# Layer 3 of a fused graph network: another score product, other stage order, held instructions

## The chip, the core and the metric

The kernel runs on one core of one Trainium2 chip. The core has a matrix engine (PE, whose weight loads are listed apart as PEld), a vector engine (DVE), a scalar engine for activations (ACT), a general engine (POOL, also called GpSimd) and a queue engine (SP) that issues DMAs. Each engine takes its instructions in order; they wait for each other by semaphores. Working memory is SBUF with 128 partitions; PE writes to PSUM, which has eight banks of 512 f32 values per partition. The metric is device time in microseconds (us).

## The reference

Four layers work on x of 128 graphs x 64 nodes x 256 features, each of them as x + layer(relu(layernorm(x))). Layer 0 is graph convolutions and small LSTMs, layer 1 attention over edges, layer 2 a dense graph layer with two batch norms, and layer 3, which the change is about, dense attention inside each graph:

```python
Wh = jnp.einsum('bnf,fo->bno', h, W)
a1, a2 = (a[:Fout, 0], a[Fout:, 0])
s1 = Wh @ a1
s2 = Wh @ a2
e = s1[:, :, None] + s2[:, None, :]
e = jnp.where(e >= 0, e, ALPHA * e)
e = jnp.where(adj_matrix[None] == 0, -jnp.inf, e)
attention = jax.nn.softmax(e, axis=-1)
h_prime = jnp.einsum('bij,bjo->bio', attention, Wh)
```

A score of nodes i and j is the sum of two half scores, s1 of the row's node and s2 of the column's node.

## The kernel before

The 8192 nodes are cut into 16 chunks (NCH) of 512: four tiles (i) of 128 nodes, which are two graphs each. All four layers run in one program; layer 3 begins when the second batch norm of layer 2 is complete. Up to that point everything is as it is after the change, but for a few tables made in late_tables during layer 0: wext (the weights W of layer 3 with W a1 as column 257), wa2 (W a2, repeated over 64 columns), eye and the mask.

A chunk passes through these functions in layer 3:

- **fetch**: a DMA on SP's queue brings the residual from memory into the tile xts[n].
- **scale_o**: POOL applies the second batch norm to layer 2's product (two instructions per chunk); the result o lies with features on the partitions.
- **second_norm**: a generator in two stages. PE turns o into nodes on the partitions (eight transposes), DVE adds it to the residual and takes the statistics of the layer norm (four pairs of bn_stats and bn_aggr). Then the roots: for chunks 1 and 2 by ACT and DVE, for all others by POOL, which also writes the normed h. Chunk 0 has its own first_norm, in halves.
- **features**: PE turns h back (eight transposes), ACT writes the relu of it as hT, in two halves.
- **project3**: hT times wext, two f32 products for each of four tiles; ACT copies each result to wh (256 values and the half score s1).
- **dense_scores**: the half scores s2 of all nodes of a graph, spread over the partitions, come from wa2 and hT (four products with 64 weight columns; the two graphs of a tile go to the two halves of the partitions). DVE adds s1, applies the leaky relu, adds the mask and takes the negative maximum (four instructions), ACT takes exp tile by tile with row sums den, DVE the reciprocal of den.
- **turn**: PE transposes the four tiles of e; DVE copies the first graph's half into fields[n % 2] and ACT the second's.
- **dense_values**: four products of the field with wh, then four DVE instructions that scale by 1/den and add the residual, then the store on SP's queue (the last chunk is stored in two halves).

PSUM is used in two kinds of buffers in this layer: "bank" (one bank, four buffers) for project3, dense_scores and turn, and "pair" (two banks, two buffers) for second_norm, features and dense_values. A buffer is used again when its last readers are done.

The order of instructions on an engine is made by a scheduler when the program is built: it takes them by readiness and by their place in the code. late(ins) holds one instruction behind the one that was traced just before it on the same engine; instructions without it may be moved. In layer 3, before the change, only chunk 0 and parts of chunks 1 and 2 are held. The main loop of iteration n runs second_norm(n+2), scale_o(n+4), features(n+1), half of project3(n), turn(n-1), the other half, dense_scores(n) and dense_values(n-1).

Of the kernel before, what the change touches and what calls it, by code (L numbers as in the profile page):

```python
# [9 lines left out]
F32 = mybir.dt.float32  # L10
# [21 lines left out]
def gnn_stack_kernel(ctx: ExitStack, tc: tile.TileContext, a: dict, out: bass.AP):  # L32
# [168 lines left out]

    tab2 = ctx.enter_context(tc.tile_pool(name="tab2", bufs=1))
    bdH = tab2.tile([P, P], F32, tag="bdH", name="bdH")
    wext = tab2.tile([P, 2, D + 1], F32, tag="wext", name="wext")
    wa2 = tab2.tile([P, 2, T], F32, tag="wa2", name="wa2")
    mask3 = tab2.tile([P, T], F32, tag="mask3", name="mask3")

    def late_tables():
        with ExitStack() as setup:
# [7 lines left out]
            late(nc.vector.tensor_scalar(mask3, adj2, 0.0, NEG, ALU.is_equal, ALU.mult))  # L217
            yield

            eye = s2.tile([P, T], F32, tag="eye", name="eye")  # L220
            for h in range(2):
                r = slice(h * T, (h + 1) * T)
                nc.vector.tensor_copy(eye[r, :], ident[r, r])
            an = s2.tile([P, T], F32, tag="an", name="an")
            anT = s2.tile([P, T], F32, tag="anT", name="anT")
            nc.vector.tensor_tensor(an, adj2, eye, ALU.add)
# [1276 lines left out]
    with ExitStack() as l2:  # L1503
# [407 lines left out]
        def second_norm(n):  # L1911

            xt, v = xts[n], hs[n][0]
            o = os3.pop(n)
            p = pair_bank()
            for i in range(4):
                for c in range(2):
                    k = (i % 2 * 2 + c) * P
                    ins = nc.tensor.transpose(p[:, i // 2, k : k + P], o[:, c, i * P : (i + 1) * P], ident)  # L1919
# [12 lines left out]
            nm = stat.tile([P, 4], F32, tag="ln_nm", name="ln_nm")  # L1932
            if n < 3:
                keep(nc.scalar.activation(rs, mv[:, :, 1], AF.Sqrt, bias=eps))
                keep(nc.vector.reciprocal(rs, rs))
                keep(nc.vector.scalar_tensor_tensor(nm, mv[:, :, 0], -1.0, rs, ALU.mult, ALU.mult))
            else:
                nc.gpsimd.tensor_scalar(rs, mv[:, :, 1], 1e-5, None, ALU.add)
                nc.gpsimd.tensor_tensor(rs, rs, half_power, ALU.pow)
                nc.gpsimd.tensor_tensor(nm, mv[:, :, 0], rs, ALU.mult)  # L1940
                nc.gpsimd.tensor_scalar(nm, nm, -1.0, None, ALU.mult)
            h = norms[n] = as_tokens(v)
            for i in range(4):
                if n > 2 or i > 1:
                    nc.gpsimd.tensor_scalar(
                        h[:, i, :], xt[:, i, :], rs[:, i : i + 1], nm[:, i : i + 1], ALU.mult, ALU.add
                    )
                else:
                    nc.scalar.activation(
                        h[:, i, :], xt[:, i, :], AF.Identity, bias=nm[:, i : i + 1], scale=rs[:, i : i + 1]  # L1950
                    )

        def features(n):

            h = norms.pop(n)
            p = pair_bank()
            for i in range(4):
                for c in range(2):
                    k = i % 2 * 2 * P + c * P
                    nc.tensor.transpose(p[:, i // 2, k : k + P], h[:, i, c * P : (c + 1) * P], ident)  # L1960
            hT = hT3[n] = t2.tile([P, 2, CHUNK], F32, tag="aggT2", name="hT3")
            for b in range(2):
                nc.scalar.activation(
                    hT[:, :, b * 256 : (b + 1) * 256].rearrange("p c (i t) -> p i c t", i=2),
                    p[:, b, :].rearrange("p (i c t) -> p i c t", i=2, c=2),
                    AF.Relu,
                )

        def project3(n, tiles):

            if n not in att3:
                wh = t4.tile([P, 4, D + 1], F32, tag="wh", name="wh", bufs=3)
                att3[n] = [wh, None, None]
            for i in tiles:
                p = bank()
                for k in range(2):
                    mm(
                        p[:, : D + 1],
                        hT3[n][:, k, i * P : (i + 1) * P],
                        wext[:, k, :],  # L1980
                        k == 0,
                        k == 1,
                    )
                nc.scalar.copy(att3[n][0][:, i, :], p[:, : D + 1])

        def dense_scores(n):

            wh, hT = att3[n][0], hT3.pop(n)
# [7 lines left out]
            nc.vector.tensor_tensor(  # L1996
                e,
                p[:, : 4 * T].rearrange("p (i t) -> p i t", t=T),
                wh[:, :, D:].to_broadcast([P, 4, T]),
                ALU.add,  # L2000
            )
            nc.vector.scalar_tensor_tensor(e, e, 0.2, e, ALU.mult, ALU.max)
            nc.vector.tensor_tensor(e, e, mask3.unsqueeze(1).to_broadcast([P, 4, T]), ALU.add)
            nmx = stat.tile([P, 4], F32, tag="nmx3", name="nmx3")
            nc.vector.tensor_reduce(nmx, e, AX.X, ALU.max, negate=True)
# [5 lines left out]
            nc.vector.reciprocal(den, den)  # L2011
            att3[n][1:] = [e, den]

        def turn(n):
# [1 line left out]
            e = att3[n][1]  # L2016
            p = bank()
            for i in range(4):
                nc.tensor.transpose(p[:T, i * P : (i + 1) * P], e[:, i, :], ident)
            f = att3[n][1] = fields[n % 2]  # L2020
            for h in range(2):
                r = slice(h * T, (h + 1) * T)
                (nc.scalar.copy if h else nc.vector.tensor_copy)(
                    f[r, :, r], p[:T, :].rearrange("p (i j) -> p i j", i=4)[:, :, r]
                )

        def dense_values(n):
            wh, f, den = att3.pop(n)
            xt = xts.pop(n)
            p = pair_bank()  # L2030
            for i in range(4):
                mm(p[:, i // 2, i % 2 * D : (i % 2 + 1) * D], f[:, i, :], wh[:, i, :D])
            for i in range(4):
                nc.vector.scalar_tensor_tensor(
                    xt[:, i, :],
                    p[:, i // 2, i % 2 * D : (i % 2 + 1) * D],
                    den[:, i : i + 1],
                    xt[:, i, :],
                    ALU.mult,
                    ALU.add,  # L2040
                )
# [5 lines left out]
            if n < NCH - 1:  # L2047
                nc.sync.dma_start(out=token_tiles(out, n), in_=xt)

        for n in range(4):  # L2050
            fetch(n)
        for n in range(3):
            scale_o(n)
        start = first_norm()
        next(start)
        second = second_norm(1)
        next(second)
        for _ in start:
            pass
        project3(0, (0, 1))  # L2060
        for _ in second:
            pass
        scale_o(3)
        for n in range(NCH + 1):
            if 4 <= n + 4 < NCH:
                fetch(n + 4)
            if n + 2 < NCH:
                for _ in second_norm(n + 2):
                    pass
            if n + 4 < NCH:  # L2070
                scale_o(n + 4)
            if n == 0:
                project3(0, (2, 3))
                dense_scores(0)
                features(1)
                continue
            if n + 1 < NCH:
                features(n + 1)
            if 0 <= n < NCH:
                project3(n, (0, 1))  # L2080
            if n >= 1:
                turn(n - 1)
            if 0 <= n < NCH:
                project3(n, (2, 3))
                dense_scores(n)
            if n >= 1:
                dense_values(n - 1)

# [1 line left out]
def _laid_out(i):  # L2090
# [65 lines left out]
```

## Time and profile before

| what | value |
|---|---|
| median of 3 runs | 1998.3 us (1996.55 to 1998.84) |
| profiled execution, its own time | 2002.48 us |
| its span | 2000.6 us |
| PE, PEld busy | 1952.1 us (98%), 1390.4 us (69%) |
| DVE, ACT, POOL busy | 1309.3 us (65%), 1139.8 us (57%), 439.3 us (22%) |
| layer 3's own part | from about 1846 us of the span to its end |

The profile is taken in one execution, which takes a little longer than the median of the runs. "Busy" is the time in which an engine has an instruction under way. A view of the profile that is cut to a stage shows what that stage is limited by, while the shares above are means over four layers. In the chain of waits each piece is the work that the end of the program was waiting for at that time. In the timeline, brackets tell how long the engine was idle before an instruction and who released it.

### The profile page before, as it was taken

Reading aid. Unit: us, or ns where it says so; the run is one execution under the profiler, and the core shown is the slowest. Engines: PE = TensorE matmul, PEld = TensorE weight load, DVE = VectorE, ACT = ScalarE, POOL = GpSimd, SP = SyncE. Lnnn points to the kernel's source line nnn. Section 1 sums busy time; section 2 is a strip of 40 time slices with the busy share of each in tenths; the row PEclk is TensorE's granted clock in tenths of the full one; section 3 lists DMA queues with packets and bytes.
Section 4 is the critical chain, followed back from the end, with each engine's and each line's share of the span. In section 5 each row is a group of like instructions: output and inputs, shape, how many; then the busy total and the mean of one; then the engine's idle time right before and its main releaser. Section 6 shows DMA issues by size and latency. Waiting matters only on the chain. (4 is left out here: it accounts for less than half of the span.)

```text
span 2000.6 us, 25691 instructions
## 1 busy us (share of the span) xinstructions
PE 1952.1 (98%) x9502; PEld 1390.4 (69%) x9502; DVE 1309.3 (65%) x2468; ACT 1139.8 (57%) x2137; POOL 439.3 (22%) x574
## 2 busy tenths in 40 slices
PE   9999999999999999999999999999999999999998
PEld 7777478866678854888666888666556775444786
DVE  8764676565475567665645655657766877886775
ACT  4343766565465547665555655567665556691544
POOL 3000031030030011310300200356654510000562
PEclk9999999999999999999999999999999999999999
DMA  8522000010010053001001000531334741022112
GB/s 271 166 69 85 0 22 1 1 42 0 1 43 0 1 190 104 22 1 43 0 1 42 1 0 17 201 105 58 117 121 152 295 154 44 0 84 84 43 54 74
DMA packets 63870, 135.61 MB, mean 68 GB/s; under 512 B 6657, under 2 KB 41345, under 8 KB 61441
## 3 DMA queue, kind: packets, MB, share of 16 engines
q1 hardware_dynamic: 59808, 124.33, 18.3%
q0 software_dynamic: 3328, 9.44, 1.3%
q8 instruction: 75, 1.23, 0.3%
q10 hardware_dynamic: 608, 0.20, 0.1%
q14 instruction: 51, 0.41, 0.1%
HBM read 87.55 MB, written 46.40 MB: 67 GB/s over the span
## 5 line engine op out<-in xcount | busy, mean ns | idle before, releaser
L761 ACT ACTIVATE gate<-gate,bias 128x256 f32<-128x256 f32 (+2 forms) x368 | 247.2, 678 | 183.6 <-DVE gate L777 100.1
L733 PE MATMUL pa<-xop,sih 128*128 128x256 f32 (+2 forms) x1056 | 342.4, 417 | 9.1 <-DVE gate L787 8.9
L733 PEld LDWEIGHTS pa<-xop,sih 128*128 128x128 f32 x1056 | 198.8, 190 | 82.5 <-issue 20.3
L733 PE MATMUL pc<-xop,wih 128*128 128x256 f32 (+2 forms) x736 | 251.1, 423 | 0.0
L777 DVE TENSOR_TENSOR gate<-pb,gate 128x256 f32<-128x256 f32 (+2 forms) x184 | 87.3, 475 | 224.7 <-PE pb L733 151.3
L733 PE MATMUL pa<-lstm_h,shh 128*128 128x256 f32 (+1 forms) x672 | 212.7, 398 | 0.0
L733 PEld LDWEIGHTS pc<-xop,wih 128*128 128x128 f32 x736 | 139.8, 190 | 51.2 <-issue 22.5
L1101 ACT ACTIVATE lr<-pair 128x1024 f32<-128x1024 f32 x128 | 124.1, 1021 | 70.5 <-PE pair L1091 40.8
L792 DVE TENSOR_TENSOR gate<-pc,gate 128x256 f32<-128x256 f32 (+2 forms) x184 | 87.4, 475 | 112.8 <-PE pc L733 112.5
L733 PEld LDWEIGHTS pa<-lstm_h,shh 128*128 128x128 f32 x672 | 127.7, 190 | 30.2
L733 PE MATMUL pc<-lstm_h,whh 128*128 128x256 f32 (+1 forms) x448 | 141.8, 398 | 0.0
L776 ACT COPY gate<-pa 128x256 f32<-128x256 f32 (+2 forms) x184 | 75.9, 412 | 91.4 <-PE pa L733 91.0
L1060 PE MATMUL bank<-wlv,hT 128*128 128x260 f32 x480 | 122.2, 398 | 0.0
L787 DVE TENSOR_TENSOR gate<-pa,gate 128x256 f32<-128x256 f32 (+2 forms) x184 | 87.2, 474 | 43.3 <-PE pa L733 42.7
L761 ACT ACTIVATE gate<-pa,bias 128x256 f32<-128x256 f32 (+2 forms) x184 | 93.7, 509 | 31.3 <-PE pa L733 29.8
L1060 PEld LDWEIGHTS bank<-wlv,hT 128*128 128x128 f32 x480 | 87.3, 192 | 32.8 <-issue 15.7
L781 ACT COPY gate<-pa 128x256 f32<-128x256 f32 (+2 forms) x184 | 75.0, 408 | 52.6 <-PE pa L733 51.6
L733 PE MATMUL pa<-xop,wih 128*128 128x256 f32 (+1 forms) x320 | 101.6, 399 | 2.8 <-ACT xop L714 2.7
L733 PE MATMUL pb<-xop,wih 128*128 128x256 f32 (+1 forms) x320 | 100.4, 398 | 0.0
L733 PEld LDWEIGHTS pc<-lstm_h,whh 128*128 128x128 f32 x448 | 85.1, 190 | 20.1
L505 POOL TENSOR_TENSOR shh<-whh 128x512 f32<-128x512 f32 x6 | 8.2, 1367 | 384.9 <-DMA whh<-in_WhhT 326.6
L784 ACT COPY gate<-pc 128x256 f32<-128x256 f32 (+2 forms) x136 | 57.7, 424 | 52.4 <-PE pc L733 51.9
(372 smaller groups left out, 3968.0 us busy)
## 6 DMA issues: line engine op xcount, KB each, us to landing
field<-keep SPq DMA_DIRECT2D x4, 2304.0 KB
wih<-in_WihT SPq DMA_DIRECT2D x8, 1024.0 KB
xres<-in_x SPq DMA_DIRECT2D x16, 512.0 KB
xa<-xres POOLq DMA_DIRECT2D x16, 512.0 KB
dense<-field SPq DMA_DIRECT2D x4, 2048.0 KB
xin<-xb SPq DMA_DIRECT2D x16, 512.0 KB
h<-xb SPq DMA_DIRECT2D x16, 512.0 KB
xin<-in_x SPq DMA_DIRECT2D x15, 512.0 KB
```

What stands on the lines that cost most here:

```text
L505: keep(nc.gpsimd.tensor_tensor(o, x, y, op))
L733: ins = nc.tensor.matmul(p[:, : self.N], weights[kind, self.phase](k, q), x[k], start=first_ and kind == "ih", stop=kind == "hh" or not se ...
L761: nc.scalar.activation(out, in_, AF.Tanh if q == 2 else AF.Sigmoid, bias=bias[:, self.w - 1, 2 * q + j : 2 * q + j + 1],)
L776: nc.scalar.copy(blk[0, 0], pa[:, :N])
L777: nc.vector.tensor_tensor(blk[0, 0], pb[:, :N], blk[0, 0], ALU.add)
L781: nc.scalar.copy(blk[1, 0], pa[:, :N])
L784: (nc.vector.tensor_copy if not self.t and self.w > 1 else nc.scalar.copy)(blk[1, 1], pc[:, :N])
L787: nc.vector.tensor_tensor(blk[1, 1], pa[:, :N], blk[1, 1], ALU.add)
L792: nc.vector.tensor_tensor(blk[1, 0], pc[:, :N], blk[1, 0], ALU.add)
L1060: ins = nc.tensor.matmul(o, hTs[n][:, k, i * P : (i + 1) * P], wlv[:, k, cols], start=k == 0, stop=k == 1)
L1101: nc.scalar.activation(lr, p, AF.Relu)
```

## The change

It touches layer 3 alone. dense_scores gets s2 another way: wext has a further column (W a2), so wh carries both half scores; a new stage, spread, lets POOL multiply s2 of each node by a unit matrix (eye), and one product with same_graph (ones inside each graph's block) puts the sums on all partitions. The main loop is rewritten: the normed chunks run three ahead instead of two, values follow two behind instead of one, and nearly all first instructions of a group on PE, and the DVE instructions, are held with late(). The sqrt of chunks 1 and 2 is issued with the statistics, ahead of the generator's second yield; a single exp of one column is put behind the sqrt of chunk 2; the reciprocal of den goes from dense_scores to dense_values; chunk 13's values are cut in halves around the end of the loop.

```diff
-    wext = tab2.tile([P, 2, D + 1], F32, tag="wext", name="wext")
-    wa2 = tab2.tile([P, 2, T], F32, tag="wa2", name="wa2")
+    wext = tab2.tile([P, 2, D + 2], F32, tag="wext", name="wext")
+    same_graph = tab2.tile([P, P], F32, tag="same_graph", name="same_graph")
+    eye = tab2.tile([P, T], F32, tag="eye", name="eye")
...
+            nc.vector.memset(same_graph, 0.0)
             for h in range(2):
                 r = slice(h * T, (h + 1) * T)
                 nc.vector.tensor_copy(eye[r, :], ident[r, r])
+                nc.vector.memset(same_graph[r, r], 1.0)
...
-                nc.vector.tensor_copy(wext[:, c, D:], p[:, 2 * c : 2 * c + 1])
-                nc.vector.tensor_copy(wa2[:, c, :], p[:, 2 * c + 1 : 2 * c + 2].to_broadcast([P, T]))
+                nc.vector.tensor_copy(wext[:, c, D:], p[:, 2 * c : 2 * c + 2])
...
         def second_norm(n):
...
-                    if n < 3 and i + c == 0:
+                    if i + c == 0:
                         late(ins)
             flat = xt.rearrange("p i d -> p (i d)")
-            keep = late if n < 3 else lambda ins: ins
-            keep(nc.vector.tensor_tensor(flat, p.rearrange("p b d -> p (b d)"), flat, ALU.add))
+            keep = late
+            late(nc.vector.tensor_tensor(flat, p.rearrange("p b d -> p (b d)"), flat, ALU.add))
+            yield
...
             rs = stat.tile([P, 4], F32, tag="ln_rs", name="ln_rs")
+            if n < 3:
+                keep(nc.scalar.activation(rs, mv[:, :, 1], AF.Sqrt, bias=eps))
             yield
...
         def features(n):
...
+                    if i + c == 0:
+                        late(ins)
...
+        def spread(n):
+
+            wh = att3[n][0]
+            hT3.pop(n)
+            across = spreads[n] = t4.tile([P, 4, T], F32, tag="across", name="across")
+            late(nc.gpsimd.tensor_tensor(
+                across,
+                wh[:, :, D + 1 :].to_broadcast([P, 4, T]),
+                eye.unsqueeze(1).to_broadcast([P, 4, T]),
+                ALU.mult,
+            ))
+
         def dense_scores(n):
...
-            for k in range(2):
-                hv = hT[:, k, :].rearrange("p (i o t) -> p o i t", o=2, t=T)
-                for h in range(2):
-                    mm(p[h * T : (h + 1) * T, : 4 * T], wa2[:, k, :], hv[:, h], k == 0, k == 1)
+            late(nc.tensor.matmul(p[:, : 4 * T], same_graph, across.rearrange("p i t -> p (i t)"), start=True, stop=True))
...
         def turn(n):
...
-                nc.tensor.transpose(p[:T, i * P : (i + 1) * P], e[:, i, :], ident)
+                ins = nc.tensor.transpose(p[:T, i * P : (i + 1) * P], e[:, i, :], ident)
+                if not i:
+                    late(ins)
...
+        def dense_values(n, tiles=(0, 1, 2, 3)):
...
+            if tiles[0] == 0:
+                results[n] = pair_bank()
+            p = results[n]
+            for i in tiles:
+                ins = nc.tensor.matmul(
+                    p[:, i // 2, i % 2 * D : (i % 2 + 1) * D], f[:, i, :], wh[:, i, :D], start=True, stop=True
                 )
+                if i in (0, tiles[0]):
+                    late(ins)
+            if tiles[0] == 0:
+                late(nc.vector.reciprocal(den, den))
+            for i in tiles:
+                late(nc.vector.scalar_tensor_tensor(
...
         for n in range(4):
             fetch(n)
             scale_o(n)
+        begun = first_norm()
+        next(begun)
+        coming = second_norm(1)
+        next(coming)
+        next(coming)
+        run(begun)
         project3(0, (0, 1))
+        run(coming)
+        coming = second_norm(2)
+        next(coming)
+        project3(0, (2, 3))
+        spread(0)
+        next(coming)
+        loaded = stat.tile([P, 1], F32, tag="loaded", name="loaded")
+        late(nc.scalar.activation(loaded, eps, AF.Exp))
+        features(1)
+        dense_scores(0)
+        run(coming)
+        scale_o(4)
+        coming = second_norm(3)
+        next(coming)
+        for n in range(1, NCH + 2):
+            if n + 3 < NCH:
+                fetch(n + 3)
+            if 1 < n <= NCH:
+                dense_scores(n - 1)
+            next(coming, None)
+            if n < NCH:
+                project3(n, (0, 1, 2, 3))
+                spread(n)
+            run(coming)
             if n + 4 < NCH:
                 scale_o(n + 4)
+            if n == NCH - 1:
+                dense_values(n - 2, (0, 1))
+                turn(n - 1)
                 continue
+            if n == NCH:
+                dense_values(n - 3, (2, 3))
+            if n == 1:
+                features(2)
+            if n >= 2:
+                dense_values(n - 2)
+            if n <= NCH:
+                turn(n - 1)
+            if n + 3 < NCH:
+                coming = second_norm(n + 3)
+                next(coming)
+            if 1 < n < NCH - 1:
+                features(n + 1)
```

run(stage) advances a generator to its end. The instructions of dense_scores on DVE, and the copies of turn, are held as well.

More of the change, by code (lines that the diff above doesn't have):

```diff
@@ L218, in late_tables @@
             yield
-            eye = s2.tile([P, T], F32, tag="eye", name="eye")
+            nc.vector.memset(same_graph, 0.0)
             for h in range(2):
@@ L1933, in second_norm @@
             if n < 3:
-                keep(nc.scalar.activation(rs, mv[:, :, 1], AF.Sqrt, bias=eps))
                 keep(nc.vector.reciprocal(rs, rs))
@@ L1959, in features @@
                     k = i % 2 * 2 * P + c * P
-                    nc.tensor.transpose(p[:, i // 2, k : k + P], h[:, i, c * P : (c + 1) * P], ident)
+                    ins = nc.tensor.transpose(p[:, i // 2, k : k + P], h[:, i, c * P : (c + 1) * P], ident)
+                    if i + c == 0:
+                        late(ins)
             hT = hT3[n] = t2.tile([P, 2, CHUNK], F32, tag="aggT2", name="hT3")
@@ L1971, in project3 @@
             if n not in att3:
-                wh = t4.tile([P, 4, D + 1], F32, tag="wh", name="wh", bufs=3)
+                wh = t4.tile([P, 4, D + 2], F32, tag="wh", name="wh", bufs=3)
                 att3[n] = [wh, None, None]
@@ L1977, in project3 @@
                     mm(
-                        p[:, : D + 1],
+                        p[:, : D + 2],
                         hT3[n][:, k, i * P : (i + 1) * P],
@@ L1983, in project3 @@
                     )
-                nc.scalar.copy(att3[n][0][:, i, :], p[:, : D + 1])
+                nc.scalar.copy(att3[n][0][:, i, :], p[:, : D + 2])
+        spreads = {}
+        def spread(n):
[8 more added lines that the diff above has]
+            ))
         def dense_scores(n):
-            wh, hT = att3[n][0], hT3.pop(n)
+            wh, across = att3[n][0], spreads.pop(n)
             p = bank()
-            for k in range(2):
-                hv = hT[:, k, :].rearrange("p (i o t) -> p o i t", o=2, t=T)
-                for h in range(2):
-                    mm(p[h * T : (h + 1) * T, : 4 * T], wa2[:, k, :], hv[:, h], k == 0, k == 1)
+            late(nc.tensor.matmul(p[:, : 4 * T], same_graph, across.rearrange("p i t -> p (i t)"), start=True, stop=True))
             e = t4.tile([P, 4, T], F32, tag="e3", name="e3")
-            nc.vector.tensor_tensor(
+            late(nc.vector.tensor_tensor(
                 e,
                 p[:, : 4 * T].rearrange("p (i t) -> p i t", t=T),
-                wh[:, :, D:].to_broadcast([P, 4, T]),
+                wh[:, :, D : D + 1].to_broadcast([P, 4, T]),
                 ALU.add,
-            )
-            nc.vector.scalar_tensor_tensor(e, e, 0.2, e, ALU.mult, ALU.max)
-            nc.vector.tensor_tensor(e, e, mask3.unsqueeze(1).to_broadcast([P, 4, T]), ALU.add)
+            ))
+            late(nc.vector.scalar_tensor_tensor(e, e, 0.2, e, ALU.mult, ALU.max))
+            late(nc.vector.tensor_tensor(e, e, mask3.unsqueeze(1).to_broadcast([P, 4, T]), ALU.add))
             nmx = stat.tile([P, 4], F32, tag="nmx3", name="nmx3")
-            nc.vector.tensor_reduce(nmx, e, AX.X, ALU.max, negate=True)
+            late(nc.vector.tensor_reduce(nmx, e, AX.X, ALU.max, negate=True))
             den = stat.tile([P, 4], F32, tag="den3", name="den3")
@@ L2010, in dense_scores @@
                 )
-            nc.vector.reciprocal(den, den)
             att3[n][1:] = [e, den]
@@ L2022, in turn @@
                 r = slice(h * T, (h + 1) * T)
-                (nc.scalar.copy if h else nc.vector.tensor_copy)(
+                late((nc.scalar.copy if h else nc.vector.tensor_copy)(
                     f[r, :, r], p[:T, :].rearrange("p (i j) -> p i j", i=4)[:, :, r]
-                )
[L2027 to L2034, printed above, removed]
+                ))
+        def dense_values(n, tiles=(0, 1, 2, 3)):
+            wh, f, den = att3[n]
+            xt = xts[n]
+            if tiles[0] == 0:
[4 more added lines that the diff above has]
+                    p[:, i // 2, i % 2 * D : (i % 2 + 1) * D], f[:, i, :], wh[:, i, :D], start=True, stop=True
+                )
+                if i in (0, tiles[0]):
[4 more added lines that the diff above has]
+                late(nc.vector.scalar_tensor_tensor(
                     xt[:, i, :],
@@ L2040, in dense_values @@
                     ALU.add,
-                )
+                ))
                 if n == NCH - 1 and i % 2:
@@ L2046, in dense_values, with run @@
                     )
-            if n < NCH - 1:
-                nc.sync.dma_start(out=token_tiles(out, n), in_=xt)
+            if tiles[-1] == 3:
+                if n < NCH - 1:
+                    nc.sync.dma_start(out=token_tiles(out, n), in_=xt)
+                for held in (att3, xts, results):
+                    held.pop(n)
+        results = {}
+        def run(stage):
+            for _ in stage:
+                pass
         for n in range(4):
             fetch(n)
-        for n in range(3):
@@ L2053, in gnn_stack_kernel @@
             scale_o(n)
[L2054 to L2059, printed above, removed]
-        project3(0, (0, 1))
[L2061 to L2069, printed above, removed]
+        begun = first_norm()
+        next(begun)
@@ L2070, in gnn_stack_kernel @@
+        next(coming)
[9 more added lines that the diff above has]
+            run(coming)
             if n + 4 < NCH:
                 scale_o(n + 4)
[L2072 to L2075, printed above, removed]
+            if n == NCH - 1:
+                dense_values(n - 2, (0, 1))
+                turn(n - 1)
@@ L2076, in gnn_stack_kernel @@
                 continue
-            if n + 1 < NCH:
-                features(n + 1)
[L2079 to L2087, printed above, removed]
+            if n == NCH:
[4 more added lines that the diff above has]
+                dense_values(n - 2)
```

## The prediction

> **What bounds the kernel now.** The page first: PE is busy for 98% of the span, so I looked for the stage that the change touches and for what fills PE there. Layer 3's own part starts at 1846.5 us. The windows view gives, for the stretch in which chunks follow each other evenly:
>
> ```profile
> 1866.00:1974.00 108.00, 107.80 (x650) 86.25 (x647) 84.00 (x235) 53.62 (x187) 71.12 (x125) 1.00 0.18 59
> ```
>
> The columns are length, then busy time of PE, weight loads, DVE, ACT and POOL, the granted clock and DMA. PE has no gap at all; DVE fills 78%, POOL 66%. The chain of waits in order of time says what PE does in one chunk (start, us, what; a "pass" is one record, and an f32 product takes two):
>
> ```profile
> 1877.12 1.93 PE pair L51 x8
> 1879.05 0.87 PE pair L1919 x8
> 1879.92 1.30 PE bank L51 x6
> 1881.23 0.87 PE pair L1960 x8
> 1882.10 0.44 PE bank L51 x2
> 1882.54 0.44 PE bank L2019 x4
> 1882.97 2.75 PE bank L51 x16
> 1885.73 1.93 PE pair L51 x8
> ```
>
> From 1877.12 to 1885.73 one chunk takes **8.61 us**, and every link is PE. In order: value products (v), the transposes of second_norm (o), six passes of project3 (p), the transposes of features (f), two passes of p, turn, the last eight passes of p and eight score passes, then v of the next chunk. Sixteen passes of p at 1.74/8 are 3.48; scores have 2.75 - 1.74 = 1.01.
>
> The six passes between o and f matter most below. The timeline shows why they stand there:
>
> ```profile
> 1879.18 1.65 DVE L2034 SCALAR_TENSOR_TENSOR h<-pair,den,h 128x256 f32<-128x256 f32 x4
> ...
> 1881.06 1.04 PE L1960 MATMUL pair<-ident,h 128*128 128x128 f32 x8
> ...
> 1882.20 1.09 ACT L1963 ACTIVATE hT<-pair 128x512 f32<-128x512 f32 x2 [0.99 <-PE pair L1960]
> ```
>
> v, o and f share two "pair" buffers in PSUM in this order, so f writes where the v before it was, and may start only when DVE has read all of v: 1879.18 + 1.65 = 1880.83. PE came there at 1881.06, 0.2 us later, thanks to the six passes. ACT in turn starts hT 1.14 us after f's start, after all eight transposes, and this hT is used a whole chunk later.
>
> The end of the kernel shows two more things:
>
> ```profile
> 1992.34 3.41 PE L51 MATMUL pair<-wh,field 128*128 128x256 f32 x8 [0.90 <-ACT field L2023]
> ...
> 1995.84 1.66 DVE L2034 SCALAR_TENSOR_TENSOR h<-pair,den,h 128x256 f32<-128x256 f32 x4 [3.95 <-PE pair L51]
> ```
>
> DVE idled until the last of the eight passes, though the first two of four tiles were ready about 1.7 us before: a reader of a pair waits for the whole pair. And this v took 3.41 instead of 1.74 us: the granted clock was 0.50 from 1992 to 1995.
>
> **What PE saves.** Eight score passes (1.01 us) become one product of ones, 128x256, two passes at 1.735/8: 0.43. Saved 0.58. The v after the scores has 1.93 here, while eight passes are 1.735 elsewhere (p after v: 1.74 for eight): 0.19 go with the change from 64 to 128 weight columns. [...] I take the row: 0.77 a chunk, 16 x 0.77 = 12.3 us of PE work. One more column in wext costs 16 x 0.217/257, 0.01 a chunk. PE's work per chunk: 0.43 + 3.48 + 1.74 + 0.44 + 0.87 + 0.87 = **7.83**.
>
> **What the order costs.** late() holds an instruction behind the one traced before it on its engine. After the change the first instruction of every group on PE is held, so PE's order in iteration n is that of the code: scores(n-1), p(n), v(n-2), turn(n-1), o(n+3), f(n+1). f(n+1) is now followed by scores(n) and p(n+1), which needs the hT of this very f. So two waits appear.
>
> (a) From the end of v to f stand only turn and o, 0.44 + 0.87 = 1.31. DVE needs 0.16 to start and 1.65 for four tiles (recip is moved ahead), PE 0.05 to follow: 1.86. PE stands 0.55.
> (b) f, then hT 1.14 after f's start, then p. The first hT of the stage started at 1853.48 and p at 1854.11: 0.63 for one half. So p starts 1.77 after f, and f and scores cover 0.87 + 0.43 = 1.30. PE stands 0.47.
>
> They close a ring: f to p 1.77, p 3.48, v 1.74 + 0.16, DVE 1.65, 0.05: **8.85 us** against 7.83 of work and 8.61 before. Nothing else is later: DVE after v has turn's copy 0.45, the add 1.25, four score operations 2.06 (rows of L1996 to L2005), statistics 2.30 (in held order, as at 1853.57 to 1855.86) and recip 0.2, 6.26 in all, and v is there after 7.2. Holding v's results behind the statistics is therefore free. [...] I take the ring, since each of its links has a row.
>
> **POOL.** spread is a two-input 128x256 operation. Rows of this size have 0.73 (L156) and, with the engines contending, 1.59 (L722); I take 0.73, as a row free of other waits. POOL then has 4 x 0.65 (h), 2 x 0.76 (o), 2.05 (roots with gaps) + 0.73 = 6.9 of 8.85. spread can start 0.6 after p ends, and scores come 1.74 + 1.86 + 0.87 = 4.47 after it: 1.59 would be hidden as well. SP: the sixteen loads h<-xb were all issued by 1843.4, ahead of every store, so their new place costs nothing; held behind stores, they would still have 9 us, and the one at 1843.07 in the chain took 3.5. The small memsets in late_tables lie in layer 0 on DVE: nothing.
>
> **The start.**
>
> ```profile
> 1853.48 1.22 ACT L1891 ACTIVATE hT<-bank 128x512 f32<-128x512 f32 x2
> ...
> 1854.11 2.00 PE L51 MATMUL bank<-wext,hT 128*128 128x257 f32 x8
> ...
> 1856.42 0.30 ACT L1934 ACTIVATE ln_rs<-ln_mv,eps 128x4 f32<-128x4 f32 x1
> ```
>
> second_norm(1) is now advanced twice before the rest of first_norm, so its root (L1934) stands ahead of hT(0) on ACT, and hT(0) is held behind it. The root needs the statistics, which end at 1855.86. So hT(0) goes from 1853.48 to 1856.2 and p(0) from 1854.11 to 1856.85, o(2) ends at 1859.45, DVE's add(2) starts at 1859.6 instead of 1857.04. From there DVE is a chain without a gap: add 1.25, statistics 2.30, e(0) 2.06, roots 0.38, add 1.25, statistics 2.30, copy 0.45, add 1.25, e(1) 2.06, statistics 2.30, recip 0.2, v(0)'s results 1.65 = 17.45, plus 0.25 of small waits: 1877.3. v(0) started on PE at 1868.44 before; the extra chunk ahead is p(2) + o(4) = 4.35 more work done by then, two chunks' scores 1.2 less, so 1871.6 would be even; it is 1873.7, **2.1 lost**. The exp table: one load, 1.28 in the trace (1862.09 to 1863.37). It leaves the way to the first exp, but that feeds turn(0), which PE reaches only at 1868.5: worth 0; should it delay hT(1) by its whole length, that is still ready before p(1) would miss more than 1 us.
>
> **The rest.** v(0)'s results end at 1877.3, v(10)'s ten rings later at 1965.8. From n = 13 on there is no o, so f no longer writes where v was; a chunk then has 1.77 + 3.48 + 1.74 + 0.44 = 7.43. p(15) ends at 1965.8 + 0.05 + 2 x 7.43 + 1.77 + 3.48 = 1985.96; before it was 1986.2. Thus all of PE's saving has gone into waits. Then half of v(13) and turn(14), 1.31, hide spread(15); scores(15); DVE is free at 1988.3 after v(13)'s half and a copy; e(15) 1.85 to 1990.15; held behind it v(13)'s second half, recip and v(14), 2.7, to 1992.9 (exp and turn(15) are done by 1992.0, so this filling costs 0.9); copies 0.9; v(15) at **1993.85** instead of 1992.34. Its clock: PE's last dense products end at 1990.6, idle for 3.3 but for transposes, as before (1989.0 to 1992.34). By that row the clock is half again and v takes 3.41; at full clock it would be 1.74. I take the row. 1993.85 + 3.50 + 1.66 + 3.1 (as from 1997.5 to 2000.6) = 2002.1, **1.5 over the span of 2000.6**. The profiled execution took 2002.48 with 1.9 around the span; the median of the runs is 1998.3. I add the difference: **1999.8**.
>
> **Rivals.** A: PE stays the bound. The last three tiles of v and the inner transposes are not held and could be put into the gaps; then ten rings lose 1.02 each: 1989.6. Against it: in gap (a) nothing is ready, and v's buffer comes free at gap (b)'s very end (copy 0.45 and add 1.25 after DVE's v). Chance 0.18. B, slower: p waits for both halves of hT, not one. Then f to p takes 1.14 + 1.09 + 0.03 = 2.26, and thirteen chunks pay 0.49: 6.4, 2006.2. It decides from the first p that starts later than 2.1 us after its f. For it: a pair's readers wait for all of it; against: 1854.11 lies before the end of the second half, 1854.70. Chance 0.18. C: the last product meets the full clock, 1.7 less, 1998.1; this lies in the forecast's own range, 1996 to 2003.5. The forecast has 0.60; 0.04 is left to a mixture on the slow side.
>
> **Numbers.** What a measurement can tell from no change is 0.2%, 4 us: 1994.3 to 2002.3. Forecast: 0.02 faster, 0.47 same, 0.11 slower; A 0.18 faster; B and the rest 0.22, of which 0.21 slower. The range runs from A's time to just over B's.
>
> **What would show it.** Right: a repeating PE gap at f released by L2034 near 0.55, one at p released by ACT hT near 0.47, chunks 8.85 apart, hT(0) after 1856, v(15) near 1994. Wrong: chunks at 7.9 to 8.1 (A), or at 9.3 (B), or chunks bound by DVE with no gap on it.

## The result and the profile after

The changed kernel takes **2006.5 us** (median of 8 runs, 2004.37 to 2009.91) beside 1998.57 for the kernel before (8 runs, 1996.55 to 2003.38): a ratio of 1.0040, 95% interval 1.0028 to 1.0052, thus some 8 us slower. The forecast was 1999.8; the measured time lies inside its range, but near the upper end, which stood just over rival B's 2006.2.

The windows view for the even stretch of layer 3, with the columns of before (length; busy PE, weight loads, DVE, ACT, POOL; granted clock, DMA share, GB/s):

```profile
1866.00:1974.00 108.00, 97.90 (x545) 81.91 (x544) 88.50 (x229) 49.52 (x184) 73.82 (x132) 1.00 0.16 54
```

PE, which had no gap, now stands 10 of 108 us, at the full clock. DVE has 82%, POOL 68%: no other engine has become full either. Such a picture can mean a ring of waits, and the timeline of one chunk shows its links (start, duration, engine and line, and in brackets the idle time before and its releaser):

```profile
1950.79 1.09 PE L1963 MATMUL pair<-ident,h 128*128 128x128 f32 x8 [0.50 <-DVE h L2059]
1951.98 1.08 ACT L1968 ACTIVATE hT<-pair 128x512 f32<-128x512 f32 x2 [0.52 <-PE pair L1963]
1952.63 3.76 PE L51 MATMUL bank<-wext,hT 128*128 128x258 f32 x16 [0.31 <-ACT hT L1968]
1956.22 1.89 PE L2051 MATMUL pair<-wh,field 128*128 128x256 f32 x8
1958.20 1.66 DVE L2059 SCALAR_TENSOR_TENSOR h<-pair,den,h 128x256 f32<-128x256 f32 x4 [1.27 <-PE pair L2051]
...
1959.92 1.09 PE L1963 MATMUL pair<-ident,h 128*128 128x128 f32 x8 [0.49 <-DVE h L2059]
```

Read from f to the next f: f to p 1.84, p to v 3.59, v to DVE's results 1.98, these and the step back to f 1.72: **9.13 us**, where a chunk of the kernel before took 8.61. Both gaps that the prediction named are there, at 0.50 and 0.31. p starts 0.65 after ACT began hT, before its second half is done (1.08): it waits for one half.

The brackets alone don't give the time lost. A PE record runs on past the point at which its successor can start: in x3 below f is 1.04 long, and the next group starts 0.88 behind it. Counted as the prediction counts, from start to start less the work between, f stands 0.65 late (3.70 from v to f, less 1.74, 0.44 and 0.87) and p 0.54 (1.84 less 0.87 and 0.43).

The start of layer 3 (the first line is its first transposes, the last its first value products, v(0)):

```profile
1844.24 1.13 PE L1845 MATMUL bank<-ident,o 128*128 128x128 f32 x8 [0.67 <-DVE o L1834]
...
1853.21 0.30 ACT L1934 ACTIVATE ln_rs<-ln_mv,eps 128x4 f32<-128x4 f32 x1 [2.32 <-DVE ln_mv L1931]
1853.41 1.06 ACT L1892 ACTIVATE hT<-bank 128x512 f32<-128x512 f32 x2
1854.04 2.78 PE L51 MATMUL bank<-wext,hT 128*128 128x258 f32 x8 [2.66 <-ACT hT L1892]
1856.61 1.91 PE L1920 MATMUL pair<-ident,o 128*128 128x128 f32 x8
...
1858.56 1.22 DVE L1925 TENSOR_TENSOR h<-pair,h 128x1024 f32<-128x1024 f32 x1 [4.65 <-PE pair L1920]
...
1870.22 0.70 PE L2009 MATMUL bank<-across,same_graph 128*128 128x256 f32 x2 [1.40 <-POOL across L1998]
...
1874.24 1.89 PE L2051 MATMUL pair<-wh,field 128*128 128x256 f32 x8
```

hT(0) stands behind the root on ACT, and PE waits 2.66 us for it. New is what comes then: the eight passes of p(0) take 2.78 instead of 2.00, the eight transposes of o(2) 1.91 instead of 1.03 (the granted clock is 0.50 from 1856 to 1858), and the second score product waits 1.40 for its spread.

The end:

```profile
1997.04 1.99 PE L2051 MATMUL pair<-wh,field 128*128 128x256 f32 x8 [1.55 <-ACT field L2039]
1999.13 1.66 DVE L2059 SCALAR_TENSOR_TENSOR h<-pair,den,h 128x256 f32<-128x256 f32 x4 [2.45 <-PE pair L2051]
```

The last product ran at the full clock (1.00 from 1997 to 1999), 1.99 instead of 3.41 before.

One warning for all comparisons below. Executions differ by some us in the layers before layer 3, which these edits touch only in a few tables of layer 0: layer 3's first transposes on PE start at 1847.10 in the profile of before, 1844.24 after. So beside the ratios I give **layer 3's own time**, from these transposes to the end of the span: 153.5 us before (1847.10 to 2000.6), 159.7 after (1844.24 to 2003.9), 6.2 more. It comes from one execution and varies too: the same changed kernel has 159.7 and, in a second profile (x12), 160.8.

### The profile page after: what moved, and what is told of

It is laid out like the page before. It is cut to its first block, busy times and chain, and to the rows that moved or that the text cites. A ratio compares the mean times of both kernels' runs of the same rounds, so it can differ in the third digit from the quotient of the medians.

```text
span 2003.9 us, 25514 instructions
## 1 busy us (share of the span) xinstructions
PE 1944.0 (97%) x9406; PEld 1390.7 (69%) x9406; DVE 1317.9 (66%) x2469; ACT 1136.8 (57%) x2138; POOL 447.9 (22%) x590
```

## Experiments

All were timed in rounds with the kernel before on the same chip. "Period" is the distance of two chunks in the even stretch, read from the starts of v.

The ratios of several variants are so near to that of the change that the intervals overlap (x1, x6, x7, x8 and x9; x2's touches it). Where the text gives a difference for these, it rests in the main on the profiles.

| kernel | ratio to before (95%) | period, us | layer 3's own time, us |
|---|---|---|---|
| before | 1 | 8.61 | 153.5 |
| the change | 1.0040 (1.0028 to 1.0052) | 9.13 | 159.7 |
| the change again (x12) | 1.0041 (1.0027 to 1.0054) | 9.13 | 160.8 |
| early hT(0) (x1) | 1.0025 (1.0016 to 1.0034) | 9.13 | 156.7 |
| f amid p (x2) | 1.0022 (1.0016 to 1.0029) | 7.88 and 9.37 in turn | 157.1 |
| f in banks (x3) | 0.9963 (0.9949 to 0.9976) | 7.98 | 146.2 |
| score product alone in before (x4) | 1.0294 (1.0280 to 1.0308) | uneven | 211.7 |
| f in banks, early hT(0) (x5) | 0.9951 (0.9937 to 0.9964) | 7.98 | 140.5 |
| f amid p, root behind spread (x6) | 1.0035 (1.0023 to 1.0047) | 8.72 | 158.1 |
| drain not filled (x7) | 1.0050 (1.0036 to 1.0064) | 9.13 | 161.2 |
| no early exp (x8) | 1.0063 (1.0049 to 1.0076) | 9.13 | 164.6 |
| old scores in the change (x9) | 1.0049 (1.0035 to 1.0062) | 9.33 | 161.9 |
| old scores in x5 (x11) | 0.9995 (0.9986 to 1.0003) | 8.61 | 150.2 |

### Is the ring the bound? Cut it at the buffer (x3)

```diff
-            p = pair_bank()
-            ...
             for b in range(2):
+                p = bank()
+                for i in (2 * b, 2 * b + 1):
+                    for c in range(2):
+                        ... transpose(p[:, k : k + P], h[:, i, ...], ident)
```

> features writes two single banks instead of a pair, in its old place at the end of the iteration. The order on PE is not touched. Ring theory: wait (a), 0.50 a chunk for DVE's results of v, goes at once since f no longer needs a pair; the way f to p gets shorter too, since ACT can start on the first bank after four of eight transposes (about 0.5 earlier): the ring is cut at DVE, and what is left is PE's own 7.83 plus what is left of (b), thus 8.0 to 8.4 apart, 7 to 11 us faster than the changed kernel. If only (b) had been the price: about 3 to 4 us. Rival (DVE or POOL is the bound): the period stays at 9 or above. What could spoil it: f then takes two of the four banks, which p and the scores also need, and p may wait for a bank (more than 0.3 at p, released by ACT's copy of wh).

Measured: 0.9963, so 15 us faster than the change by the ratios and 13.5 in layer 3's own time. Its timeline:

```profile
1912.46 1.04 PE L1965 MATMUL bank<-ident,h 128*128 128x128 f32 x8
1913.16 0.60 ACT L1968 ACTIVATE hT<-bank 128x512 f32<-128x512 f32 x1 [2.61 <-PE bank L1965]
1913.34 0.60 PE L2009 MATMUL bank<-across,same_graph 128*128 128x256 f32 x2
1913.81 3.76 PE L51 MATMUL bank<-wext,hT 128*128 128x258 f32 x16
...
1917.41 1.89 PE L2051 MATMUL pair<-wh,field 128*128 128x256 f32 x8
...
1920.44 1.04 PE L1965 MATMUL bank<-ident,h 128*128 128x128 f32 x8
```

From f to the next f it is 7.98. PE has no bracket any more: f needs no pair that v held, and ACT begins its first half 0.70 after f's start instead of 1.19, so p follows in 1.35 instead of 1.84. No engine was relieved of any work; the two buffers alone gave 1.15 us a chunk. They cut the ring in two places at once, at DVE and in the way from f to p; how the 1.15 divides between these wasn't tried. The whole gain is above what I expected, since eleven chunks times 1.15 are 12.7, and the last ones gain as well. DVE or POOL as the bound are excluded: the same work now fits in 7.98.

### The same ring cut by order, and what took its place (x2, x6)

```diff
-                project3(n, (0, 1, 2, 3))
+                project3(n, (0, 1))
+                if 1 < n < NCH - 1:
+                    features(n + 1)
+                project3(n, (2, 3))
...
-            if 1 < n < NCH - 1:
-                features(n + 1)
```

> features(n+1) moves from the end of iteration n to the middle of project3(n), as in the kernel before. Same work, same number of pairs and banks. Ring theory: f now writes where a v of two chunks earlier was, and hT is ready some 5 us before p needs it, so both waits (0.50 for DVE's results of v, 0.31 for ACT's hT) go; the chunks come 7.9 to 8.2 us apart instead of 9.13 (PE's work 7.83, DVE's 7.94), the kernel is 9 to 12 us faster than the changed one, about 1995 to 1997. Rival (DVE or POOL with their work of a chunk have become the bound, and the waits on PE only show it): the period stays at 9 or above and the time within 2 us of the changed kernel. Rival (only the clock or the start is the loss): no change.

Measured: 1.0022, by the ratios only 3.6 us faster than the change and by layer 3's own time 2.6, where 9 to 12 was expected: a miss. Both of the ring's waits are gone, but in every second chunk PE waits for POOL. The timeline of x2:

```profile
1912.31 0.23 POOL L1941 TENSOR_SCALAR ln_rs<-ln_mv 128x4 f32<-128x4 f32 x1 [3.02 <-DVE den L2057]
1912.62 1.04 POOL L1942 TENSOR_TENSOR ln_rs<-ln_rs,half_power 128x4 f32<-128x4 f32 x1
...
1914.24 0.61 POOL L1998 TENSOR_TENSOR across<-wh,eye 128x256 f32<-128x256 f32 x1
...
1914.90 0.70 PE L2009 MATMUL bank<-across,same_graph 128*128 128x256 f32 x2 [1.27 <-POOL across L1998]
```

The scheduler put the roots ahead of the spread, and POOL stood idle for 3.02 before them, until DVE was through with the statistics and den. So x6 holds the first root behind the spread:

```diff
-                nc.gpsimd.tensor_scalar(rs, mv[:, :, 1], 1e-5, None, ALU.add)
+                late(nc.gpsimd.tensor_scalar(rs, mv[:, :, 1], 1e-5, None, ALU.add))
```

> The version with features in the middle of project3 had no wait left for DVE or ACT at f and p, but its chunks came 7.9 and 9.4 us apart in turn: in every second one the score product waited 1.3 us for the spread, which stood behind the four root instructions on GpSimd. Here the first root instruction is held behind the spread, nothing else. Ring theory: what was left was that queue alone, so the period becomes even, 7.9 to 8.1, the waits of the score product for the spread (10.3 us in 9 times there) fall under 2 us in all, and the kernel is about 7 us faster than that version, about 1996 to 1998 beside 2000.6 for the kernel before. Rival (DVE's statistics, which the roots wait for, set the alternation): the period stays near 8.6 on average and the time within 2 us of that version.

Measured: 1.0035, a miss on both sides. The waits of the score product are gone and the period is even, but it is 8.72, not 8.0: a third ring. Its waits on PE, by the waits view cut to 1866 to 1990 (in total, times, longest):

```profile
PE pair L1963 <- POOL h L1948: 4.8, 16, 0.5
```

f now waits for the normed h, piece by piece: from its start to p's second half it takes 1.75 (1918.25 to 1920.00) instead of 0.87. h waits for the roots, these for the spread, the spread for all of wh, and wh's last copies stand on ACT behind the four exps, until 1923.2, though the second half of p, which follows f, began at 1920.00 and takes 1.91. This ring is read from the trace; no run cuts it. With f amid p, neither of the two orders tried on POOL reached the 7.98 of x3.

### Is PE's saving worth anything in this order? (x9, x11)

```diff
-            late(nc.tensor.matmul(p[:, : 4 * T], same_graph, across...))
+            for k in range(2):
+                hv = hT[:, k, :].rearrange("p (i o t) -> p o i t", o=2, t=T)
+                for h in range(2):
+                    ... matmul(p[h * T : (h + 1) * T, : 4 * T], wa2[:, k, :], hv[:, h], ...)
```

(The edit also puts wa2 back among the tables and takes the multiplication out of spread.)

> The changed kernel in its whole order, but the half scores again by the eight narrow passes of the kernel before, from hT; GpSimd spreads nothing. PE has 0.58 to 0.77 a chunk more to do. If the ring is the bound, these passes stand in the stretch between f and p, where PE waits for hT anyway: f and passes take 0.87 + 1.01 = 1.88 there, and the link f to p has 1.84. So the period goes from 9.13 to between 9.15 and 9.4 (the drain of the array at the change of columns included), 0.3 to 4 us in all: PE's saving, for which the change was made, is worth next to nothing in this order. Rival (PE's work still counts): the period grows by the full 0.58 to 0.77, to 9.7 or 9.9, and the kernel gets 9 to 12 us slower.

Measured: period 9.33, 0.20 more, ratio 1.0049 beside 1.0040. In its timeline the old passes stand where PE would have waited:

```profile
1908.76 1.09 PE L1962 MATMUL pair<-ident,h 128*128 128x128 f32 x8 [0.50 <-DVE h L2057]
1909.79 1.08 PE L2003 MATMUL bank<-hT,wa 128*64 128x256 f32 x8
1910.80 3.76 PE L51 MATMUL bank<-wext,hT 128*128 128x258 f32 x16
```

The bracket (b) ahead of p is gone and (a) is as before. The same exchange in x5, where no ring is left (the two edits of x3 and x1 with the old scores):

> The version with features in banks and the early hT(0), whose chunks come 7.98 apart with PE full, but the half scores again by the eight narrow passes; GpSimd spreads nothing. In the changed kernel this exchange cost 0.20 a chunk (9.13 to 9.33). Theory: with the ring cut PE is the bound, so the passes now count in full, 0.58 to 0.77 less the 0.15 by which PE's 7.83 lies under 7.98: a period of 8.4 to 8.6, and 6 to 10 us slower than that version, about even with the kernel before or up to 3 us faster. Rival (DVE's 7.94 sets the 7.98, PE has room): the period stays under 8.2 and the time within 3 us of that version.

Measured: period 8.61 instead of 7.98, ratio 0.9995 instead of 0.9951: 0.63 a chunk and 8.8 us in all. PE is busy in all of the window from 1866 to 1964 in both:

```profile
1866.00:1964.00 98.00, 98.00 (x561) 85.30 (x560) 87.34 (x233) 52.27 (x185) 77.55 (x137) 1.00 0.19 65
1866.00:1964.00 98.00, 98.00 (x591) 81.71 (x590) 84.81 (x219) 48.74 (x175) 62.71 (x112) 1.00 0.17 60
```

The first line is x5's, the second x11's. One chunk of x11 on PE:

```profile
1904.64 1.04 PE L1964 MATMUL bank<-ident,h 128*128 128x128 f32 x8
1905.61 1.08 PE L2003 MATMUL bank<-hT,wa 128*64 128x256 f32 x8
1906.62 3.76 PE L51 MATMUL bank<-wext,hT 128*128 128x258 f32 x16
1910.22 1.89 PE L2049 MATMUL pair<-wh,field 128*128 128x256 f32 x8
```

The score product is worth 0.63 a chunk where PE is the bound and 0.20 inside the ring. And 8.61 is the period of the kernel before, which had PE full with the old scores: the order of the change, even with its ring cut, gains nothing of itself in the even stretch.

### Why the new order is needed at all (x4)

The kernel before with the score product, the wider wext and the spread (not held), all in its old order:

```diff
-            for k in range(2):
-                ... wa2 passes
+            across = t4.tile([P, 4, T], F32, tag="across", name="across")
+            nc.gpsimd.tensor_tensor(across, wh[:, :, D + 1 :]..., eye..., ALU.mult)
+            mm(p[:, : 4 * T], same_graph, across...)
```

> The kernel before with one part of the change alone: the half scores ride in the projection as one more column, GpSimd spreads them and one product of ones replaces the eight narrow passes. Order, waits held by hand, chunks ahead and the drain are those of before. Work on PE falls by 0.58 a chunk, and by 0.77 if the extra 0.19 of the product after the scores goes as well. Theory 1 (PE stays the bound and its queue has other work to put ahead of the scores): 9 to 12 us faster than before, about 1987 to 1989. Theory 2 (the scores stand directly behind the projection, so they wait for ACT's copy, 0.6, and the spread, 0.7, less what the last tile hides): each chunk loses about 1.3 and wins 0.77, and the kernel is 5 to 10 us slower than before, about 2004 to 2008, with a repeating wait of the score product for POOL's spread. That would be the reason for which the change needs chunks three ahead at all.

Measured: 1.0294, some 60 us slower. The second theory has the right sign and is far too small. The waits view from 1866 to 2030, and one such wait in the timeline:

```profile
PE bank L51 <- POOL across L1992: 31.9, 13, 3.8
```

```profile
1936.39 1.52 POOL L1908 TENSOR_SCALAR o<-h,scale,shift 128x512 f32<-128x512 f32 x2
1937.87 0.62 POOL L1992 TENSOR_TENSOR across<-wh,eye 128x256 f32<-128x256 f32 x1
1938.55 0.70 PE L51 MATMUL bank<-across,same_graph 128*128 128x256 f32 x2 [3.61 <-POOL across L1992]
```

I had counted the spread's own 0.7, not POOL's queue: the roots (until 1934.14), four h (2.17) and two o (1.52) stood ahead of it. These waits are 31.9 us in 13 times; turn's waits for the exps are another 7.9 in the same window, and the mean clock from 1866 to 1990 fell to 0.90. How the rest divides wasn't tried.

### The start (x1, x5)

```diff
         next(coming)
-        next(coming)
         run(begun)
+        next(coming)
         project3(0, (0, 1))
```

> Only the start is put back: hT(0) stands ahead of the root of second_norm(1) on ACT. Nothing else is touched. My theory (the start costs some 5 us: p(0) waits 2.66 us for hT(0), and the pause lets the granted clock fall to 0.50 just after it, which makes p(0) and o(2) another 2 us longer): p(0) starts near hT(0)'s first half without a wait over 1 us, its eight passes take about 2.0 and not 2.78, o(2) about 1.05 and not 1.91, the ring of 9.13 us stays as it is, and the kernel is 3 to 5 us faster than the changed one (about 2002). Rival (DVE's work in the first chunks sets the beat there and PE's pauses cost nothing): less than 1.5 us faster. Rival (the clock falls anyway, whatever stands before): p(0) still takes 2.8, and 1 to 2 us are won.

Measured: 1.0025, 3.0 us faster than the change by the ratios and by layer 3's own time. p(0) in its timeline:

```profile
1853.14 2.01 PE L51 MATMUL bank<-wext,hT 128*128 128x258 f32 x8
1854.99 1.04 PE L1920 MATMUL pair<-ident,o 128*128 128x128 f32 x8
```

No wait, and the full clock (1.00 in every us from 1851 to 1857). From layer 3's first transposes to v(0) it takes 25.75 us (1845.93 to 1871.68) instead of 30.00 (1844.24 to 1874.24): 4.25 at the start. The profiled execution gave 1.24 of it back at the end, where v(15) took 3.23 (granted clock 0.54 from 1995 to 1996, 0.50 from 1996 to 1998).

> Two edits together: features in two single banks (the period fell from 9.13 to 7.98 with it) and hT(0) ahead of the root on ACT (p(0) then came without its wait of 2.66 and at the full clock). If start and ring are two separate losses, as I hold, the two gains add up: 3 us for the start under the version with banks alone, thus about 1990 and 8 to 11 us faster than the kernel before. Rival (with the ring gone, DVE's 7.94 of work a chunk is the bound, and a start that comes earlier on PE only waits for DVE): within 1 us of the version with banks alone.

Measured: 0.9951, by the ratios 2.4 us better than x3, with intervals that overlap; in the profile v(0) starts 24.26 us after the first transposes instead of 29.89 in x3. So the two gains add up where layer 3 is looked at alone; by the medians it is shown less well. x5 is the fastest kernel here, 9.8 us under the kernel before.

### The two small parts (x7, x8, x12)

x7 leaves dense_values(13) whole:

```diff
-                dense_values(n - 2, (0, 1))
+                dense_values(n - 2)
...
-            if n == NCH:
-                dense_values(n - 3, (2, 3))
```

> The changed kernel with its drain not filled: the value products of chunk 13 stay whole and in their place, ahead of turn(14). Theory of the prediction (the filling hides the spread of chunk 15, but its held results stand before v(14)'s on DVE and cost as much): within 1 us of the changed kernel. Rival 1 (the filling is worth its 1.3 us of PE work ahead of scores(15)): 1 to 2 us slower. Rival 2 (v(13)'s second half waits for the read of its first half, 0.3 at PE, and stands in DVE's way): 1 us faster or more.

Measured: 1.0050, the interval overlapping that of the change; the times don't decide. In the profiles v(12) to v(15) takes 16.48 us (1985.48 to 2001.96) instead of 15.01 (1982.03 to 1997.04; the same 15.01 in x12): the filling is worth 1.5 there, as rival 1 has it and not the prediction's theory.

x8 leaves out the early exp:

```diff
-        loaded = stat.tile([P, 1], F32, tag="loaded", name="loaded")
-        late(nc.scalar.activation(loaded, eps, AF.Exp))
```

> The changed kernel without the early exp: the table is loaded at the first exp of the scores. Prediction's step: worth 0, since the first exp feeds turn(0), which PE reaches later; within 1 us of the changed kernel run beside it, ring and all else the same. Rival: the load's 1.28 us stands on the way to turn(0) or to hT(1) and shows in full, 1.3 us slower, or more if PE's clock falls again.

> The changed kernel once more, beside the two others, as their measure: 1.003 to 1.005 of the kernel before, chunks 9.13 apart. If p(0)'s slow clock is due to the pause before it, it shows again here: p(0) at 2.7 us or more after a wait of 2.66.

Measured: x12 as before, 1.0041. x8 has 1.0063: by the ratios 4.4 us slower than x12, with intervals that overlap, and 3.8 in layer 3's own time. So the theory (within 1 us) fails. The rival is right that it costs more than the load and that the clock falls again, but not on the way that it named, to turn(0) or hT(1). In x8's timeline:

```profile
1865.06 1.28 ACT L2023 ACT_TABLE_LOAD   x1
...
1868.34 1.36 PE L1963 MATMUL pair<-ident,h 128*128 128x128 f32 x8 [1.07 <-ACT h L1952]
...
1874.27 0.70 PE L2009 MATMUL bank<-across,same_graph 128*128 128x256 f32 x2 [3.26 <-POOL across L1998]
1874.81 5.33 PE L51 MATMUL bank<-wext,hT 128*128 128x258 f32 x16
```

The load's 1.28 moves the exps, and behind them on ACT stands half of chunk 2's norm (L1952), for which f waits 1.07. In this program the scheduler also put four h and one o on POOL (2.17 and 0.78) ahead of the spread, which in the change stands ahead of these h. The score product waits 3.26 instead of 1.40, and after this pause the sixteen passes of p take 5.33 instead of 3.65: the mean granted clock from 1866 to 1965 is 0.98, in x12 1.00. From the first transposes to v(0): 34.98 (1845.00 to 1879.98) against 31.17 in x12 (1842.96 to 1874.13), so all of the 3.8. It is the price of this program without the early exp; how it divides between the load, POOL's other order and the clock wasn't tried.

## Why the prediction was near, and where it was off

**The ring: right in kind, 0.28 short.** It was forecast at 8.85 and is 9.13. The mis-sized terms: f to p 1.77, measured 1.84; p 3.48, measured 3.59 to v's start; v to DVE 1.90, measured 1.98. Each is small, ten rings make it 2.7 us. The gaps, forecast at 0.55 and 0.47, are 0.65 and 0.54 in the same count. x3 shows that the chunks were held by this ring: with its pair replaced by two banks they come at PE's pace. x9 and x11 show that of PE's saving of 0.63 a chunk all but 0.20 went into its waits.

**PE's saving: 0.63, not 0.77.** With PE full a chunk takes 7.98 (x5), not 7.83. Sixteen passes of p in a row take 3.60 to v's start (1913.81 to 1917.41 in x3), not twice 1.74; x11 has the same 3.60, so it isn't the new scores, and why stays open. The 0.19 that the prediction put down to the change of weight columns isn't seen at that size: in x11 the narrow passes start 0.97 behind f, in x3 the wide product 0.88, so 0.09. Inside the ring this error cost nothing of its own but p's 0.11. v takes 1.73 to the start of turn (1956.22 to 1957.95 in the change, 1917.41 to 1919.14 in x3), near the 1.74 in the sum; that its fall from 1.93 comes from the columns was the author's estimate, and no run shows a drain of the array, which x9's expectation counts in, as the cause.

**Rival A (PE stays the bound)** didn't come: no instruction moved into the gaps. (The prediction says that the first instruction of every group on PE is held; that of p is not, but the traces have it where the code has it.) Its period of 7.83 is nearly what x3 has without the ring, 7.98. **Rival B (p waits for both halves)** is refuted by p's start 0.65 after hT's; the slower time came without it.

**The start: the step that was most wrong.** Put at 2.1 us lost, it lost 5.5. hT(0)'s delay was exact: p(0) starts 9.80 us after the first transposes, forecast 9.75. Two things were missing. PE's pause there wasn't carried on to its clock, though the prediction reckoned with the half clock at the end: add(2) on DVE starts 14.32 after the first transposes instead of 12.5, 1.8 more. And the spread was costed in the even stretch alone; at the start the wait of 1.40 for it is most of the next 1.6. Putting hT(0) back ahead of the root (x1) removes PE's pause and the half clock, and with them 4.25 of the 5.5. That contending engines give the 1.59 of L722, which the prediction weighs for the spread, was the author's estimate and isn't shown: in the profile of before L156 takes 0.72 to 0.75 from 1574.60 to 1577.60 too, where DVE is busy throughout.

**The exp table: worth 0 was wrong**; the program without the early exp is some 4 us slower (4.4 by the ratios, 3.8 in the profiles). The step named what the exps feed (turn(0)), not what is queued behind them on ACT.

**The drain: right.** From the end of v(10)'s results on DVE to v(15) the forecast had 28.05 (1965.8 to 1993.85), and it took 28.04 (1969.00 to 1997.04). The filling gains 1.5 in the stretch (x7); the 0.9 that I charged for it was part of that sum, and it wasn't measured alone.

**The last product's clock: wrong**, 1.99 instead of 3.41. That was rival C's term.

**From the profile to the median.** In layer 3 alone the forecast was 1.5 more than before; with 3.4 at the start, 2.7 in the rings and 1.4 less at the end this becomes the 6.2 that the profiles show. So 4.7 of the 6.7 us between 1999.8 and 2006.5 are layer 3's. The other 2.0 lie in the baseline: the profiled execution of before was 4.2 longer than the median, and I took that off the forecast, while that of after was 0.8 shorter than its median (2005.68 beside 2006.49), 5.0 in all; against it stand the 2.9 that the layers ahead of layer 3 took less in it.

So the time fell into the range by luck: because it had been drawn to just over B's 2006.2, for a wait that didn't come, not because the middle was right.

## What to carry to other kernels

When an edit takes work from a full engine and changes its order, write the new order down and look for rings: buffer to reader to next writer, with what each queue puts between; the longest ring sets the period (here 9.13 us, and 7.98 with it cut in x3), and work saved where the engine would wait anyway gains little (here 0.20 of 0.63 us a chunk). Moving work to another engine costs that engine's queue, not only the operation: the same spread of 0.62 us was hidden in the even stretch of one order and in another made PE wait up to 3.8 us a time. A buffer shared by three stages can be worth more than the arithmetic saved: here 1.15 us a chunk, with the earlier start of ACT that came with it, against 0.63.

## What was not expected of the hardware

**The clock after a pause of PE.** In all eight profiles where p(0) waited 2.66 to 2.67 us (the change, x2, x3, x6 to x9, x12), its eight passes took 2.78 to 3.81; in the five where it didn't wait (before, x1, x4, x5, x11) 2.00 or 2.01. The windows of x12 around the pause:

```profile
1851.00:1852.00 1.00, 0.00 (x0) 0.00 (x0) 0.82 (x4) 0.07 (x1) 0.00 (x0) 0.88 0.00 0
1852.00:1853.00 1.00, 0.24 (x1) 0.24 (x2) 0.34 (x2) 1.00 (x3) 0.20 (x1) 0.50 0.00 0
...
1857.00:1858.00 1.00, 1.00 (x6) 1.00 (x6) 0.00 (x0) 0.00 (x0) 0.00 (x0) 0.50 0.00 0
1858.00:1859.00 1.00, 1.00 (x6) 0.85 (x5) 0.69 (x1) 0.00 (x0) 0.00 (x0) 0.71 0.00 0
```

And two of the first profile of the change:

```profile
1855.00:1856.00 1.00, 1.00 (x4) 0.80 (x3) 0.00 (x0) 0.71 (x2) 0.16 (x1) 0.57 0.00 0
1858.00:1859.00 1.00, 1.00 (x6) 0.94 (x5) 0.44 (x1) 0.00 (x0) 0.00 (x0) 0.73 0.00 0
```

The column before the last two is the clock. In slices of 0.1 us the change shows two values of it, 1.00 up to 1855.10 and 0.50 from 1855.20 to 1858.50. If there are only these two, a slice of one us at 0.88 was at half the clock for 0.24 us, one at 0.71 for 0.58. In x12 it was then half from 1851.76 to 1858.58, 6.82 us, though PE was full again from 1852.76. In the change the same reckoning gives 1855.14 to 1858.54, 3.40 us, and there the fall came when PE had worked again for over a us. So the same pause, of 2.66 us, had a different price in two executions of the same kernel: p(0) took 2.78 in the change and 3.81 in x12. What sets the moment of the fall and its length, these runs don't show. At the end of the kernel, after four transposes and then the same wait of 1.55, v(15) took 1.99 in the change and 3.23 in x1:

```profile
1994.49 3.23 PE L2051 MATMUL pair<-wh,field 128*128 128x256 f32 x8 [1.55 <-ACT field L2039]
```

So here pauses of 2.66 and 1.55 us were followed by the half clock, the shorter one in x1 but not in the change.
